# A state-space scan laid out as 8 batch rows x 16 states on the partitions, with its neighbouring stages cut into 4-step chunks

## The chip, the cores and the metric

The kernel runs on one core of a Trainium2 chip. A core has five engines that work from queues of their own: TensorE (PE, matrix products; its weight loads are listed as PEld), VectorE (DVE), ScalarE (ACT), GpSimd (POOL) and SyncE (SP, which here only starts DMA transfers). PE writes its products to PSUM, a small accumulator memory cut into banks; all other tiles are in SBUF, 128 partitions wide. The metric is the time of one execution in microseconds on the device, a median of several runs. Everything is in float32.

## The reference, cut to what matters

Two nets follow each other on x (128 sequences x 32 steps x 128 channels): a conditioning net and six layers of attention and feed-forward. The change is in the conditioning net alone:

```
xr, gate = split(x @ W_in.T)            # 256 channels each
xr = xr + t_emb[:, None, :]
xc = silu(causal_conv4(xr) + b_conv)    # along the 32 steps, each channel by itself
xn = layernorm(xc) * ln_g + ln_b
Bm, Cm, dt = split(xn @ W_xproj.T, 3)   # 16 states each
dt = tanh(dt @ W_dt.T + b_dt) * 0.01
Ad = 1 + dt * -tanh(A_log)
Bd = Bm * minimum(norm(xn), 1)
for each step t:                        # h: sequences x 16 states x 256 channels
    h = clip(h * Ad[t] + Bd[t] (x) xn[t], -10, 10)
    ys[t] = sum over states of Cm[t] * h
out = (ys + D * xn) * silu(gate) @ W_out.T
```

The loop is a true recurrence: with the clip in it, step t cannot start before step t-1 is clipped. One step handles 128 x 16 x 256 state values.

## The kernel before, in words

`cond_net` (lines 107 to 391) fills the stream `xT`, which holds channels on partitions and 4096 tokens along the free dimension; `ffn_net` (line 527) works on it in place. Both open their own pools of tiles, and those of `cond_net` close before those of `ffn_net` open.

`cond_net` works in three stages, one behind the other.

1. Lines 156 to 209, eight rounds of 16 sequences: load x (L161), transpose (L167), project (L172), add the embedding (L175), convolve with one ACT and three DVE operations (L183, L191), SiLU (L199); the gate likewise (L204, L205). Results have channels on partitions.
2. Lines 212 to 307, all 32 steps: transpose back to sequences on partitions (L220, L221), moments (L226, L227), normalise (L240), scale and shift (L249), transpose again (L260, L265), project to the 48 small values per token (L272, L279), squares for the norm (L283), then the small vectors Bd and Ad.
3. Lines 317 to 391, the scan. Sequences are on partitions, so h is a tile of 128 x 16 x 256, and Ad and Bd of one state are one value per partition. For each step, in groups of four states, ACT writes the products Bd (x) xn into a PSUM tile `u` with two buffers (L332), and DVE adds h_old * Ad (L339: one scalar_tensor_tensor of 128x256 for each of 16 states). After every eight states DVE clips 128x2048 values in one tensor_scalar (L349). For the read-out POOL builds 16 diagonal matrices of Cm (L355, four operations), and PE multiplies the 2 x 16 blocks of h with them and accumulates (L368), together with D * xn (L364). DVE multiplies by the gate (L373), and every fourth step PE projects (L382) and ACT copies to the stream (L391).

The order of instructions on an engine in these stages is that of the program, as the framework schedules it. `ffn_net` is different: it registers every step with a time in a `Plan` (line 394), which sorts them by time and ties each instruction to the one before it on its engine. The times set the order on each engine, nothing more: an engine starts its next instruction as soon as what it depends on is there. `ffn_net` starts with loads of weights (L449 to L478) and clearing two tiles on POOL (L440).

Other lines that the steps below refer to: L685 and L488 are tensor_scalar operations on POOL, L978 copies on POOL, L674, L691 and L743 tensor_tensor operations on POOL, all in `ffn_net`; L720 and L798 are its products on parts of the array (128 rows x 32 columns, and 32 rows x 64 columns), L817 its output projection of 256 columns.

Of the kernel before, what the change touches and what calls it, by code (L numbers as in the profile page):

```python
# [8 lines left out]
F32 = mybir.dt.float32  # L9
# [97 lines left out]
def cond_net(tc, x, cond, w_inT, w_xT, w_xdt, w_dtT, w_outT, ident, eps, pv, rv, stream):  # L107
    nc = tc.nc
    with ExitStack() as ctx:
        big = ctx.enter_context(tc.tile_pool(name="c_big", bufs=1))  # L110
        ps = ctx.enter_context(tc.tile_pool(name="c_ps", bufs=4, space=PSUM))

        wi = big.tile([128, 4, 128], F32, name="wi")
        nc.sync.dma_start(out=wi, in_=w_inT.rearrange("d (m c) -> d m c", c=128))
        wx = big.tile([128, 2, 3 * NS], F32, name="wx")
        nc.sync.dma_start(out=wx, in_=w_xT.rearrange("(k p) n -> p k n", p=128))
        wxd = big.tile([NS, C], F32, name="wxd")
        nc.scalar.dma_start(out=wxd, in_=w_xdt)
        wdt = big.tile([NS, NS], F32, name="wdt")
        nc.scalar.dma_start(out=wdt, in_=w_dtT)  # L120
        wot = big.tile([128, 2, 128], F32, name="wot")
        nc.sync.dma_start(out=wot, in_=w_outT.rearrange("(k p) n -> p k n", p=128))
        cd = big.tile([128, C], F32, name="cd")
        nc.scalar.dma_start(out=cd, in_=cond)


        gT = big.tile([128, 2, S, B], F32, name="gT")

        xcT = big.tile([128, 2, S, B], F32, tag="chan", name="xcT")

        condT = big.tile([128, 2, B], F32, name="condT")
        pc = ps.tile([128, 512], F32, tag="mm", name="pc")
        for ct in range(2):
            nc.tensor.transpose(
                pc[:, ct * 128 : (ct + 1) * 128], cd[:, ct * 128 : (ct + 1) * 128], ident
            )
        nc.vector.tensor_copy(condT, pc[:, :256].rearrange("p (k b) -> p k b", k=2))


        wc = big.tile([128, 2, 3 * NS], F32, name="wc")  # L140
        nc.vector.tensor_copy(wc[:, :, 0 : 2 * NS], wx[:, :, 0 : 2 * NS])
        pw = ps.tile([128, 512], F32, tag="mm", name="pw")
        for ct in range(2):
            nc.tensor.matmul(
                pw[:, ct * NS : (ct + 1) * NS],
# [950 lines left out]
```

## Time and profile before

| what | value |
|---|---|
| median of 3 runs | 3165.16 us (3161.58 to 3169.61) |
| the profiled execution, first to last instruction | 3171.8 us, that is 6.6 us above the median |
| busy: PE, PEld, DVE, ACT, POOL | 2994.4, 2033.4, 2632.2, 2201.3, 2114.7 us |
| conditioning net, stages 1 and 2 | about 0 to 145 us |
| conditioning net, scan | about 145 to 483 us |
| first attention product of the feed-forward net | 489.2 us |
| mean granted TensorE clock | 0.98 of full |

The page's 40 slices show the busy tenths of each engine; a slice is 79 us, so the conditioning net is the first six:

```profile
PE   6678886999999999999999999999999999999998
DVE  6699996888888888888888888888888888888884
ACT  6577773777776777777777767777777777677674
POOL 0144546777777777777777777777777777777772
PEclk9699998999999999999999999999999999999999
```

In the rows of instruction groups, a line reads: line of the kernel, engine, operation, output <- inputs, shapes, count, then total busy time, mean ns of one, and the idle time of the engine just before with what ended it. The mean of one can be longer than busy time over count, because consecutive operations overlap by some 80 ns. Profiled spans on POOL are rough.

### The profile page before, as it was taken

What the parts mean: (1) busy time and instruction counts of PE and PEld (TensorE: products, weight loads), DVE (VectorE), ACT (ScalarE), POOL (GpSimd) and SP (SyncE); (2) the same over time, 40 slices, a digit from 0 to 9 for tenths busy, and PEclk for the clock granted to TensorE, in tenths of its full rate; (3) what the DMA queues carried; (4) which work ended last, traced back from release to release, by engine and by line L of the source; (5) the groups of instructions that cost most, each with busy time, mean ns of one, the idle gap of its engine ahead of it and who ended that gap; (6) DMA issues with size and microseconds to landing.
All of it is one profiled execution on the core that took longest, in us unless ns stands there. A gap on an engine that the chain in (4) does not pass through costs nothing.

```text
span 3171.8 us, 105434 instructions
## 1 busy us (share of the span) xinstructions
PE 2994.4 (94%) x47942; PEld 2033.4 (64%) x47942; DVE 2632.2 (83%) x3607; ACT 2201.3 (69%) x2656; POOL 2114.7 (67%) x1560
## 2 busy tenths in 40 slices
PE   6678886999999999999999999999999999999998
PEld 3677773666666666666666666666666666666665
DVE  6699996888888888888888888888888888888884
ACT  6577773777776777777777767777777777677674
POOL 0144546777777777777777777777777777777772
PEclk9699998999999999999999999999999999999999
DMA  1000001000001000000000010000000000000000
GB/s 45 1 1 1 1 1 60 9 3 2 2 2 33 5 2 2 2 22 13 4 2 2 2 33 5 2 2 2 22 13 8 2 3 2 2 2 9 16 9 25
DMA packets 24586, 30.21 MB, mean 10 GB/s; under 512 B 1342, under 2 KB 22348, under 8 KB 23372
## 3 DMA queue, kind: packets, MB, share of 16 engines
q1 hardware_dynamic: 23644, 22.50, 2.3%
q8 instruction: 377, 6.18, 0.8%
q10 hardware_dynamic: 496, 0.97, 0.1%
q14 instruction: 69, 0.57, 0.1%
HBM read 21.36 MB, written 2.10 MB: 7 GB/s over the span
## 4 chain that ended last, share of the span: by engine, by line
PE 86%; DVE 5%; ACT 1%; POOL 1%; issue 1%; DMA 0%; DVEq 0%; POOLq 0%; ACTq 0%; SPq 0%
PE pq L644 20%; PE po L817 11%; PE pv L776 11%; PE pt L702 10%; PE av L798 8%; PE ph L923 8%; PE sim L720 6%; PE py L368 5%; PE pf L949 4%; DVE h L339 2%; DVE h L349 2%; PE pm L901 1%; PE pt L877 1%; POOL rot L674 1%; PE po L382 1%
## 5 line engine op out<-in xcount | busy, mean ns | idle before, releaser
L674 POOL TENSOR_TENSOR rot<-rot,tmp 128x512 f32<-128x512 f32 x768 | 956.5, 1272 | 16.8 <-DVE tmp L665 16.5
L644 PE MATMUL pq<-wq_t,xT 128*128 128x512 f32 x1536 | 714.3, 598 | 9.6 <-DMA wq_t<-in_wqkv_dram 6.6
L655 ACT ACTIVATE sq<-pq 128x1024 f32<-128x1024 f32 x384 | 393.5, 1025 | 473.2 <-DVE tmp L665 467.3
L665 DVE TENSOR_TENSOR rot<-pq,rt 128x1024 f32<-128x1024 f32 x384 | 468.0, 1219 | 190.7 <-PE pq L644 185.5
L743 POOL TENSOR_TENSOR sc<-sc,tb 128x1024 f32<-128x1024 f32 x96 | 227.2, 2367 | 406.3 <-DVE sc L734 291.3
L669 DVE TENSOR_REDUCE ssq<-sq 128x16 f32<-128x1024 f32 x384 | 465.5, 1212 | 8.4 <-ACT sq L655 4.2
L665 DVE TENSOR_TENSOR tmp<-pq,rt 128x1024 f32<-128x1024 f32 x384 | 466.3, 1214 | 0.0
L644 PEld LDWEIGHTS pq<-wq_t,xT 128*128 128x128 f32 x1536 | 278.3, 192 | 254.0 <-issue 239.3
L702 PE MATMUL pt<-ident,rot 128*128 128x128 f32 x3072 | 374.4, 275 | 24.6 <-POOL rot L691 22.3
L702 PEld LDWEIGHTS pt<-ident,rot 128*128 128x128 f32 x3072 | 344.3, 142 | 76.9 <-issue 28.6
L712 ACT COPY kd<-pt 64x1024 f32<-64x1024 f32 x384 | 387.0, 1008 | 4.9 <-PE pt L702 2.6
L817 PE MATMUL po<-oT,wo_t 128*128 128x256 f32 x1536 | 372.3, 385 | 0.8 <-DVE hid L936 0.5
L776 PE MATMUL pv<-wq_t,xT 128*128 128x512 f32 x768 | 362.9, 605 | 0.0
L691 POOL TENSOR_TENSOR rot<-rot,rn 128x1024 f32<-128x1024 f32 x192 | 361.6, 1905 | 0.1
L798 PEld LDWEIGHTS av<-at,v 32*64 32x64 f32 x24576 | 264.5, 130 | 113.8 <-issue 69.9
L763 POOL TENSOR_TENSOR sc<-sc,sm 128x1024 f32<-128x1024 f32 x96 | 184.0, 1916 | 227.7 <-DVE sm L759 215.7
L817 PEld LDWEIGHTS po<-oT,wo_t 128*128 128x128 f32 x1536 | 284.0, 190 | 80.2 <-issue 44.5
L355 POOL TENSOR_TENSOR dg<-ident,dbc 128x512 f32<-128x512 f32 x128 | 160.0, 1282 | 238.3 <-PE py L368 179.8
L368 PE MATMUL py<-dg,h 128*128 128x128 f32 x2048 | 248.8, 280 | 67.2 <-DVE h L349 67.2
L786 ACT COPY v<-pv 128x1024 f32<-128x1024 f32 x192 | 194.2, 1012 | 169.7 <-PE pv L776 169.7
L798 PE MATMUL av<-at,v 32*64 32x32 f32 x24576 | 286.1, 225 | 7.4 <-DVE at L769 4.9
L368 PEld LDWEIGHTS py<-dg,h 128*128 128x128 f32 x2048 | 240.5, 196 | 71.7 <-issue 71.2
(129 smaller groups left out, 4376.2 us busy)
## 6 DMA issues: line engine op xcount, KB each, us to landing
wq_t<-in_wqkv_dram SPq DMA_DIRECT2D x6, 1536.0 KB, 6.9
xl<-in_x_dram SPq DMA_DIRECT2D x16, 256.0 KB, 3.0
wo_t<-in_wo_dram SPq DMA_DIRECT2D x6, 512.0 KB, 5.0
out_dram<-xl SPq DMA_DIRECT2D x8, 256.0 KB, 3.0
w_t<-in_w_dram SPq DMA_DIRECT2D x6, 341.0 KB, 5.6
w_t<-in_w_dram SPq DMA_DIRECT2D x6, 128.0 KB, 2.9
rv<-in_rvec_dram ACTq DMA_DIRECT2D x1, 656.0 KB, 4.4
wi<-in_w_inT_dram SPq DMA_DIRECT2D x1, 256.0 KB
```

The lines of the kernel that those rows point to most:

```text
L368: nc.tensor.matmul(py[:, cs], h[:, d, cs], dg[:, d, :], start=False, stop=(d == NS - 1))
L644: self.nc.tensor.matmul(self.acc[i, c][:, n, :], self.shifted(i), self.wq_t[:, o : o + 512], start=True, stop=True,)
L655: self.nc.scalar.activation(sq.rearrange("p h d -> p (h d)"), pq, AF.Square)
L665: nc.vector.tensor_tensor(out, pq, table, ALU.mult)
L669: self.nc.vector.tensor_reduce(self.ssq[:, i, c * H : (c + 1) * H], sq, AX.X, ALU.add)
L674: self.nc.gpsimd.tensor_tensor(rot[:, :, a : a + 32], rot[:, :, a : a + 32], tmp[:, :, b : b + 32], ALU.add)
L691: self.nc.gpsimd.tensor_tensor(kr, kr, rk, ALU.mult)
L702: nc.tensor.transpose(pt[:, n * 128 : (n + 1) * 128], rf[:, o : o + 128], self.net.ident)
L712: self.nc.scalar.copy(self.net.kd[i][rows, :, :, r, :], ptc[rows])
L776: self.nc.tensor.matmul(self.acc["v", i][:, n, :], self.shifted(i), self.wq_t[:, o : o + 512], start=True, stop=True,)
L798: self.nc.tensor.matmul(self.av[j // 2][64 * r : 64 * r + 64, j % 2, o : o + 32], self.v[i][toks, h * DH : (h + 1) * DH], self.at[toks, i ...
L817: self.nc.tensor.matmul(self.po, self.wo_t[:, c, :], self.oT[:, :, :, c, :].rearrange("p j i q -> p i j q"), start=(c == 0), stop=(c == HP ...
```

## The change

Stages 1 and 2 and the scan become steps of a `Plan`, as in the feed-forward net. The 32 time steps are cut into 8 chunks of 4. A `Chunk` does for its 4 steps and all 128 sequences what stages 1 and 2 did (its convolution takes the last three columns of the chunk before), and its steps have times up to 57 units ahead of its first scan step; a scan step has 8 units.

In a `Scan` step the state lies otherwise. There are 16 groups of 8 sequences; in a group, the 128 partitions are 8 sequences x 16 states, and the free dimension is the 256 channels. Per step:

- The terms Bd (x) xn are 16 products on PE, in two halves: a stationary block of 32 sequences x 128 (8 sequences x 16 states, zero where the sequence differs) times xn of these 32 sequences. Four products with different rows of the array go to four PSUM banks. The tile has one buffer.
- DVE updates with 16 scalar_tensor_tensor operations of 128x256, one for each group, with Ad as one value per partition.
- The clip is four tensor_scalar operations of 128x1024 on POOL.
- The read-out is 16 products with a stationary block of 128 x 32 (Cm placed so that each sequence sums its 16 states), four side by side in the array's columns. DVE adds D * xn, POOL multiplies by the gate, PE transposes, ACT copies, and every fourth step PE projects and ACT stores.

To make the blocks, ACT multiplies the 48 small values of a chunk by eight masks (`masked`) and four more (`spread`); PE turns Ad and Cm to the new partitions (`select`), and POOL places Cm (`placed`). The layer norm's scale and shift move from DVE to POOL, the normalisation from DVE to ACT, and the 48 small values are projected from the SiLU output before normalisation, with the norm folded into the weights and applied afterwards. The constants for this are made once at the start. `cond_net` keeps its place and its pools still close before the feed-forward net's open. Dots stand for what is left out.

```diff
-def cond_net(tc, x, cond, w_inT, w_xT, w_xdt, w_dtT, w_outT, ident, eps, pv, rv, stream):
...
+QT = 4
+NQ = S // QT
+STEP = 8
+GROUPS = B // 8
+class Cond:
...
+        self.cm = [big.tile([128, QT * 4, 160], F32, name=f"cm{i}") for i in range(2)]
+        for cm in self.cm:
+            nc.gpsimd.memset(cm.rearrange("p r w -> p (r w)"), 0.0)
...
+        plan = Plan(tc)
+        self.chunks = [Chunk(self, q) for q in range(NQ)]
+        for q in range(NQ):
+            self.chunks[q].plan(plan, q * QT * STEP)
+        for t in range(S):
+            Scan(self, t).plan(plan, t * STEP)
+        plan.emit()
...
+    def load(self, q):
+        xl = self.xl[q] = self.wk.tile([128, QT, D], F32, tag="cxl", name="cxl")
+        self.nc.sync.dma_start(out=xl, in_=self.x[:, q * QT : (q + 1) * QT, :])
+class Chunk:
...
+    def plan(self, plan, t0):
+        def at(time, step, *args):
+            plan.at(t0 + time, lambda: step(*args))
+        if self.q >= 2:
+            at(-93.31, self.load)
+        at(-56.94, self.tokens)
+        at(-55.40, self.copied)
+        at(-55.18, self.project, 0)
+        at(-55.06, self.conditioned, 0)
+        at(-53.81, self.project, 1)
+        at(-50.61, self.tap, 0)
+        at(-50.35, self.conditioned, 1)
+        at(-49.00, self.taps, 0, 0)
+        at(-45.12, self.tap, 1)
+        at(-42.59, self.taps, 1, 0)
+        at(-40.58, self.taps, 0, 1)
+        at(-38.43, self.gates, 0)
+        at(-37.76, self.taps, 1, 1)
+        at(-36.22, self.gated, 0)
+        at(-34.49, self.taps, 0, 2)
+        at(-33.64, self.taps, 1, 2)
+        at(-33.40, self.silu, 0)
+        at(-31.72, self.gates, 1)
+        at(-31.05, self.silu, 1)
+        at(-29.65, self.gated, 1)
+        at(-29.39, self.back, 0)
+        at(-29.21, self.back, 1)
+        at(-28.57, self.moments, 0)
+        at(-28.35, self.moments, 1)
+        at(-25.96, self.deviation)
+        at(-25.18, self.inverse)
+        at(-24.33, self.normalised, 0)
+        at(-23.89, self.normalised, 1)
+        at(-23.02, self.scaled, 0)
+        at(-20.95, self.offset, 0)
+        at(-20.24, self.norm, 0)
+        at(-18.50, self.scaled, 1)
+        at(-18.46, self.small, 0)
+        at(-17.23, self.small, 1)
+        at(-17.04, self.offset, 1)
+        at(-14.94, self.skip)
+        at(-14.93, self.small_out)
+        at(-13.89, self.norm, 1)
+        at(-13.71, self.norm_root)
+        at(-13.45, self.inputs)
+        at(-12.49, self.masked)
+        at(-6.15, self.select)
+        at(-5.55, self.spread, 0)
+        at(-3.67, self.decay)
+        at(-3.59, self.outputs)
+        at(-1.51, self.decays)
+        at(1.69, self.placed)
+        at(3.82, self.spread, 1)
+        at(52.20, self.project_out)
+        at(53.63, self.store)
...
+    def conditioned(self, ct):
+        nc = self.nc
+        if ct == 0:
+            self.xp = self.wk.tile([128, 2, QT + 3, B], F32, tag="xp", name="xp")
+            if self.q == 0:
+                nc.gpsimd.memset(self.xp[:, :, 0:3, :], 0.0)
+            else:
+                before = self.net.chunks[self.q - 1].xp
+                nc.gpsimd.tensor_copy(self.xp[:, :, 0:3, :], before[:, :, QT : QT + 3, :])
+        nc.vector.tensor_tensor(
+            self.xp[:, ct, 3:, :],
+            self.acc.pop(("r", ct)).rearrange("p (t b) -> p t b", b=B),
+            self.net.condT[:, ct, :].unsqueeze(1).to_broadcast([128, QT, B]),
+            ALU.add,
+        )
...
+    def taps(self, ct, k):
+        acc = self.acc["c", ct]
+        self.nc.vector.scalar_tensor_tensor(
+            acc, self.xp[:, ct, k : k + QT, :], self.weight(ct, k), acc, ALU.mult, ALU.add
+        )
...
+    def moments(self, u):
+        nc = self.nc
+        if u == 0:
+            self.stats = self.wk.tile([128, QT, 6], F32, tag="cst", name="cst")
+            self.mv = self.wk.tile([128, QT, 2], F32, tag="cmv", name="cmv")
+        for k in range(2):
+            nc.vector.bn_stats(self.stats[:, 2 * u + k, :], self.acc["t", u][:, k * C : (k + 1) * C])
+        for k in range(2):
+            nc.vector.bn_aggr(self.mv[:, 2 * u + k, :], self.stats[:, 2 * u + k, :])
...
+    def affine(self, u, o, op):
+        xn = self.xn[:, 2 * u : 2 * u + 2, :]
+        row = self.net.rv[:, o : o + C].unsqueeze(1).to_broadcast([128, 2, C])
+        self.nc.gpsimd.tensor_tensor(xn, xn, row, op)
...
+    def masked(self):
+        self.m = self.wk.tile([128, QT * 3, 8, NS], F32, tag="m", name="m", bufs=1)
+        src = self.dbc.rearrange("p t (k d) -> p (t k) d", d=NS)
+        for l in range(8):
+            self.nc.scalar.activation(
+                self.m[:, :, l, :], src, AF.Copy, scale=self.net.in_group[:, l : l + 1]
+            )
+    def spread(self, u):
+        if u == 0:
+            self.e = self.wk.tile([128, QT, 4, 128], F32, tag="e", name="e")
+        src = self.m.rearrange("p (t k) l d -> p t k (l d)", k=3)[:, :, 0, :]
+        for j in (2 * u, 2 * u + 1):
+            self.nc.scalar.activation(
+                self.e[:, :, j, :], src, AF.Copy, scale=self.net.quarter[:, j : j + 1]
+            )
+    def select(self):
+        ps = self.psel = self.net.bank("psel")[:, : QT * 2 * GROUPS].rearrange(
+            "p (k t g) -> p k t g", k=2, t=QT
+        )
+        m = self.m.rearrange("p (t k) l d -> p t k (l d)", k=3)
+        for t in range(QT):
+            for k in range(2):
+                self.nc.tensor.matmul(
+                    ps[:, k, t, :], m[:, t, 1 + k, :], self.net.of_group, start=True, stop=True
+                )
...
+    def placed(self):
+        self.cm = self.net.cm[self.q % 2]
+        dst = self.cm.rearrange("p r (m w) -> p r m w", w=40)[:, :, :, 0:8]
+        part = [128, QT * 4, 4, 8]
+        self.nc.gpsimd.tensor_tensor(
+            dst,
+            self.cs.rearrange("p t (r m) -> p (t r) m", m=4).unsqueeze(3).to_broadcast(part),
+            self.net.row_b.unsqueeze(1).unsqueeze(1).to_broadcast(part),
+            ALU.mult,
+        )
...
+class Scan:
...
+    def plan(self, plan, t0):
+        def at(time, step, *args):
+            plan.at(t0 + time, lambda: step(*args))
+        at(-1.59, self.terms, 0)
+        at(0.06, self.update, 0, 0)
+        at(0.33, self.update, 0, 1)
+        at(2.40, self.clip, 0, 0)
+        at(5.23, self.terms, 1)
+        at(5.83, self.update, 1, 0)
+        at(5.94, self.clip, 0, 1)
+        at(6.16, self.update, 1, 1)
+        at(7.68, self.clip, 1, 0)
+        at(10.84, self.clip, 1, 1)
+        at(13.52, self.read, 0)
+        at(14.38, self.read, 1)
+        at(15.75, self.skip)
+        at(19.83, self.gate)
+        at(22.42, self.turn)
+        if self.t % 2 == 1:
+            at(23.35, self.turned)
+    def terms(self, i):
+        ch, k = self.chunk, self.k
+        self.u = self.net.ps.tile([128, 4, 2, C], F32, tag="u", name="u", bufs=1)
+        for j in range(2):
+            for r in range(4):
+                rows = slice(32 * r, 32 * r + 32)
+                self.nc.tensor.matmul(
+                    self.u[:, r, j, :],
+                    ch.e[rows, k, 2 * i + j, :],
+                    ch.xn[rows, k, :],
+                    start=True,
+                    stop=True,
+                )
+    def update(self, i, w):
+        nc, net, ch = self.nc, self.net, self.chunk
+        if i == 0 and w == 0:
+            net.h[self.t] = self.wk.tile([128, 2, 4, 2, C], F32, tag="h", name="h")
+        h = net.h[self.t]
+        if self.t == 0:
+            nc.vector.tensor_copy(h[:, i, 2 * w : 2 * w + 2], self.u[:, 2 * w : 2 * w + 2])
+            return
+        for r in (2 * w, 2 * w + 1):
+            for j in range(2):
+                g = 4 * r + 2 * i + j
+                nc.vector.scalar_tensor_tensor(
+                    h[:, i, r, j, :],
+                    net.h[self.t - 1][:, i, r, j, :],
+                    ch.a[:, self.k, g : g + 1],
+                    self.u[:, r, j, :],
+                    ALU.mult,
+                    ALU.add,
+                )
+    def clip(self, i, w):
+        h = self.net.h[self.t][:, i, 2 * w : 2 * w + 2].rearrange("p r j c -> p (r j c)")
+        self.nc.gpsimd.tensor_scalar(h, h, -10.0, 10.0, ALU.max, ALU.min)
+    def read(self, i):
+        ch = self.chunk
+        if i == 0:
+            self.y = self.net.ps.tile([128, 512], F32, tag="y", name="y", bufs=1)
+        h = self.net.h[self.t]
+        for j in range(2):
+            for r in range(4):
+                m = 2 * i + j
+                self.nc.tensor.matmul(
+                    self.y[32 * r : 32 * r + 32, 0:C],
+                    ch.cm[:, self.k * 4 + r, 32 * m : 32 * m + 32],
+                    h[:, i, r, j, :],
+                    start=(m == 0),
+                    stop=(m == 3),
+                )
+    def skip(self):
+        self.z = self.wk.tile([128, C], F32, tag="z", name="z")
+        self.nc.vector.tensor_tensor(self.z, self.y[:, 0:C], self.chunk.xd[:, self.k, :], ALU.add)
+    def gate(self):
+        self.nc.gpsimd.tensor_tensor(self.z, self.z, self.chunk.g[:, self.k, :], ALU.mult)
...
```

## The prediction

> **What bounds the kernel now.** I first cut the span into stages (busy time of each engine in each stretch: busy us and count, then the granted TensorE clock). The conditioning net ends near 482.8 us; the feed-forward net behind it is not edited.
>
> ```profile
> 0.00:76.00 76.00, 45.23 (x113) 21.59 (x114) 50.01 (x77) 48.21 (x52) 5.06 (x28) 0.92 0.16 47
> 76.00:145.00 69.00, 42.88 (x255) 42.28 (x253) 51.74 (x114) 36.95 (x103) 10.36 (x8) 0.65 0.00 1
> 145.00:482.80 337.80, 270.69 (x2200) 256.85 (x2200) 304.07 (x592) 245.57 (x527) 149.61 (x120) 0.97 0.00 1
> ```
>
> DVE is busy 304 of the 337.8 us of the scan (90%), PE 271, ACT 246, POOL 150; ahead of it lie 145 us in which no engine leads. The groups of instructions by form give the prices:
>
> ```profile
> L339 DVE SCALAR_TENSOR_TENSOR h<-h,ad,u 128x256 f32<-128x256 f32 x496 | 202.4, 473 | 3.5 <-ACT u L332 3.5
> L349 DVE TENSOR_SCALAR h<-h 128x2048 f32<-128x2048 f32 x64 | 95.4, 1490 | 7.5 <-ACT h L326 5.4
> L373 DVE TENSOR_TENSOR z<-py,gT 128x256 f32<-128x256 f32 x32 | 13.6, 425 | 20.7 <-PE py L368 20.5
> L191 DVE SCALAR_TENSOR_TENSOR acc<-xp,pv,acc 128x512 f32<-128x512 f32 x48 | 33.9, 747 | 1.0 <-ACT acc L183 0.6
> ...
> L674 POOL TENSOR_TENSOR rot<-rot,tmp 128x512 f32<-128x512 f32 x768 | 956.5, 1272 | 16.8 <-DVE tmp L665 16.5
> L691 POOL TENSOR_TENSOR rot<-rot,rn 128x1024 f32<-128x1024 f32 x192 | 361.6, 1905 | 0.1
> L743 POOL TENSOR_TENSOR sc<-sc,tb 128x1024 f32<-128x1024 f32 x96 | 227.2, 2367 | 406.3 <-DVE sc L734 291.3 <-DVE sd L895 115.0
> L685 POOL TENSOR_SCALAR rn<-rn 128x64 f32<-128x64 f32 x96 | 35.1, 366 | 27.2 <-ACT rn L680 27.2
> L978 POOL COPY full<-xT 64x496 f32<-64x496 f32 x8 | 4.8, 598 | 36.2 <-DVE last L957 35.9
> L488 POOL TENSOR_SCALAR cg<-cen,pv 128x128 f32<-128x128 f32 x6 | 3.7, 612 | 0.0
> ...
> L978 POOL COPY full<-last 64x16 f32<-64x16 f32 x8 | 1.7, 213 | 0.0
> ```
>
> The timeline of one step (start, duration, engine) shows how they queue:
>
> ```profile
> 255.97 2.04 DVE L339 SCALAR_TENSOR_TENSOR h<-h,ad,u 128x256 f32<-128x256 f32 x5
> 258.04 1.82 DVE L349 TENSOR_SCALAR h<-h 128x2048 f32<-128x2048 f32 x1
> 259.78 3.21 DVE L339 SCALAR_TENSOR_TENSOR h<-h,ad,u 128x256 f32<-128x256 f32 x8
> 263.02 1.23 DVE L349 TENSOR_SCALAR h<-h 128x2048 f32<-128x2048 f32 x1
> 265.86 0.42 DVE L373 TENSOR_TENSOR z<-py,gT 128x256 f32<-128x256 f32 x1 [0.44 <-PE py L368]
> 266.20 2.04 DVE L339 SCALAR_TENSOR_TENSOR h<-h,ad,u 128x256 f32<-128x256 f32 x5
> ```
>
> The period is 266.20 - 255.97 = 10.23 us, of which DVE is busy 9.74: sixteen updates at (3.21 - 0.08)/8 = 0.39 (the last one's end does not overlap the next), 6.25, two clips of 1.23 and 1.82, one read-out product of 0.42. So **DVE bounds the scan**, and 32 x 10.2 + about 11 us at its two ends make up the 338. Last, the chain of waits shows how the stage is joined to the next:
>
> ```profile
> 480.62 2.00 PE po L382 x4
> 482.76 6.30 DMA wq_t<-in_wqkv_dram
> 489.19 3.77 PE pq L644 x4
> ```
>
> The last output product releases the load of the first attention weights, which PE waits for. The change leaves that joint: all pools of the net still close together. Everything from 482.8 on (3171.8 - 482.8 = 2689.0 us) is therefore carried over.
>
> **The change, part by part.**
>
> *The 145 us ahead of the scan* shrink to set-up and the first chunk alone; chunks 1 to 7 go beside the scan. Set-up: the trace's first matmul waits until 9.56 us for DMA; the new constants add about eight small hops between engines (four transposes of 0.28, copies of 0.6, small DVE operations of 0.2), to some 14 us. The first chunk is a chain, from rows of the same form: four transposes 1.1, copy 0.6, projection 0.85 (512 columns, as at 13 us), two sums 0.69 each, six taps 0.75 each, two SiLU 1.09 and a table load 1.28, transposes 1.1, moments 2.25 (12.5 + 5.5 us over 32), square root with load 1.5, reciprocal and offset 0.8, four normalisations 0.48 each, POOL scale and shift 4 x 1.27, squares 4 x 0.60, three small DVE operations 0.7, eight masks 0.4 each, spreads 2 x 0.8, tanh with load 1.5: 34 us, and 4 us for chunk 1 in between. The loads of x stay eight of 256 KB on SP (3.0 us to landing); all but two are now issued some 36 us ahead of their use with nothing queued before them: nothing, or 3 us where one is late. The scan then starts at about 14 + 38 = 52 us. After the last update come clip, read-out, sum, gate, two transposes, copy, two products of 0.6: 6 us. **Ends together: 58 us.**
>
> *DVE per step.* The updates keep their form (128x256, SBUF, a pointer, PSUM) and their count: 16 x 0.39 = 6.25. Clips leave: -3.05. The read-out sum stays at 0.42. New beside it, per 4-step chunk: two sums 1.38, six taps 4.24 (33.9/48 each), moments 2.25, small ones 1.5 = 9.4, or 2.35 a step. Sum 9.02.
>
> *ACT per step* loses 16 x 0.47 = 7.4 us of products. Per chunk it has copies 0.6 + 1.2, taps 1.6, SiLU 4.3, normalisations 1.9, squares 2.4, masks 3.2, spreads 3.3, stores 1.5, small 1.0, and four table loads of 1.28 (SiLU, square root and tanh alternate): 26 us, 6.5 a step. It is off the path, with 3 us to spare.
>
> *PE per step* loses 34 products of 128 columns and gets 16 of 32 rows x 128 columns (terms) and 16 of 128x32 (read-out), 256 wide, plus 1.7 us of chunk work (40 products and transposes). Such a product alone is 372.3/1536 = 0.24 us; the 32-row and 32-column forms of the attention run together at 0.012 and 0.016 us for 32 and 64 columns, two to four times below serial pace, so 8 terms take 0.9 (weight loads of 0.117 one behind another) to 1.9 us. PE needs 4 to 9.8 us. I take 5.5.
>
> *The new waits.* The term tile has a single buffer: DVE finishes eight updates, PE starts eight terms, DVE goes on. Hop, weight load and first product are 0.05 + 0.15 + 0.38 + 0.05 = 0.63 us, twice a step; where terms run serially, the fifth adds 0.6. What is queued on DVE between the two halves covers it: by the plan's times each first gap holds 1.4 to 2.25 us of chunk work and each second one the 0.42 of the read-out sum and up to 0.9. If that cover is late, up to 2 x 1.25 = 2.5 a step is lost. On PE the read-out of step t-1 stands between the two blocks of terms, so a late clip of the last piece holds the next step's first terms, and with them DVE.
>
> *POOL per step* loses the diagonals (4 x 1.28) and gets four clips of 128x1024, **the price that the trace lacks**. Around them: gate 0.73 (between 455 ns for 128 and 1272 for 512 elements), and per chunk scale and shift 5.1, skip 2.4, placing 1.3, carry-over copy 0.8: 9.6, or 2.4. So POOL = 4C + 3.1. Low end of C: the COPY rows grow by (598 - 213)/480 = 0.80 ns per element; 0.366 + 960 x 0.80 = **1.14 us**. High end: the straight line through the two TENSOR_SCALAR rows, (612 - 366)/64 = 3.84 ns per element, gives **4.05**. That line leaves 120 ns of fixed cost where COPY shows 200, and its second row reads a pointer and the first an immediate, as the clip does; so part of the difference should be the pointer. The two-input rows of the same size are 1.91 and 2.37. I take the nearest kind, one streamed input with immediates: 1.2 to 1.5, POOL 7.9 to 9.1, just under DVE. I keep both ends. The balance with DVE lies at C = (9.7 - 3.1)/4 = 1.65.
>
> The Trainium skill speaks on both sides here: its page GPSIMD Engine Reference, section Engine selection, calls GPSIMD the wrong place for elementwise work with two inputs (about half of VectorE's speed) but roughly at line rate with one, and its cycle accounting states 1.03 cycles per element for bodies of at most two operations, an estimate of 1024 x 1.03/1.2 = 0.88 us and a fixed part; by that POOL would need some 7 us a step and DVE stay the bound, while by the TENSOR_SCALAR line POOL would need 19.3. No row here shows a long one-input operation with two constants, so no run yet agrees or disagrees.
>
> *Port.* In the step above the clip that ran beside POOL took 1.82, the other 1.23: 0.6 us lost. Six taps per chunk have two SBUF inputs and may meet it: 0 to 6 x 0.6/4 = 0.9 a step. With the uncovered part of the term waits I put 0.7 on DVE's 9.02: **9.7 a step**.
>
> The Trainium skill (SBUF — State Buffer, Who interferes with whom) says that a VectorE instruction with two SBUF inputs holds off a GpSimd one that reads SBUF, and the other way round, for the whole instruction; by it a tap could wait for a full clip, 6 x 1.3/4 = 2 a step at worst, and the updates, with one input in PSUM, not at all.
>
> *Clock.* It was 0.65 at 76 to 145 us, 1.00 late in the scan and 0.85 after the joint (482.8 to 600). With less PE work in the scan it may be lower at the joint; at 0.65 for 60 us PE-bound work would lose 15 us, and as much can be gained if it is not cut at all. I put 0.
>
> **Sum.** 58 + 32 x 9.7 = 368 in place of 482.8: -114 us on the profiled 3171.8, which gives 3057. The median of the runs, 3165.2, is 6.6 lower: **3051**.
>
> **Rivals.** In general the time is 3165.2 - 482.8 + 58 + 32 x step = 2740 + 32 x step.
> (1) *The term buffer's cover is late*: step 9.0 + 1.3 to 2.5 = 10.3 to 11.5, 3070 to 3108. For it: engines take work in written order, and chunk work waits on others. Against: a chunk runs six steps ahead.
> (2) *POOL becomes the bound, mildly*: C between 1.65 and 2.5, as the two-input rows of that size have; at 1.91 the step is 10.7, 3082; at 2.37, 12.6, 3143.
> (3) *Slower: the clip on POOL costs as the TENSOR_SCALAR rows' line says.* The step that loses all is (482.8 - 58)/32 = 13.3, so it decides from C = 2.55. At 2.9: 14.7, 3210. At 4.05: 19.3, 3358. For it: both rows of that operation lie on the line, and no POOL row of it is cheap. Against: the fixed costs above.
> (4) *It doesn't do what it says*: the chunks run not beside the scan but ahead of its parts; then the 145 us stay, and 9.7 - 2.35 + 0.5 = 7.85 a step gives 3165 - 338 + 32 x 7.85 + 10 = 3088. This is unlikely, as nothing but the engines' order ties them.
>
> **Chances.** Forecast (step 9.0 to 10.3) 0.43, its own range 3028 to 3070; rivals 1 and 4 0.14; rival 2 0.10; rival 3 0.30; between, within 0.3% (9.5 us, about what a measurement can tell from no change) 0.03. Faster 0.67, same 0.03, slower 0.30. The range starts at 3015 and must take in about half of rival 3; C up to 3.3, a step of 16.3, ends at 3260.
>
> **What would show it.** After: the scan's start near 52 us and its end near 368; DVE over 90% busy between, POOL 80 to 95%; updates still 0.39 each; the clip's row on POOL below 1.65 us. If POOL is near 100% and DVE waits for it, rival 2 or 3 holds and the clip's mean tells which; if DVE waits for the term products on PE while POOL has gaps, rival 1. The forecast is wrong if C is above 1.65 or if the feed-forward part is not 2689 us.

## The result

The changed kernel takes 3316.3 us (median of 4 runs, 3316.1 to 3317.7) against 3163.8 us before (now four runs): a ratio of 1.048 (95% interval 1.046 to 1.050). It is **slower by some 152 us**, where 114 us of gain were forecast and 3260 us was the end of the range. The profiled execution spans 3314.3 us.

The same cut into stages as before, now at the scan's first update (48.9 us) and at the load that begins the feed-forward net (625.1 us); busy us and counts in the order PE, PEld, DVE, ACT, POOL, then the granted clock:

```profile
0.00:48.90 48.90, 26.04 (x105) 17.66 (x106) 21.12 (x51) 23.47 (x46) 16.52 (x21) 0.85 0.16 52
48.90:625.10 576.20, 324.39 (x2508) 173.47 (x2508) 274.07 (x685) 135.70 (x286) 553.75 (x208) 0.74 0.01 2
625.10:3314.30 2689.20, 2633.28 (x45376) 1712.53 (x45376) 2226.36 (x2824) 1871.65 (x1978) 1948.21 (x1404) 0.99 0.03 10
```

The 145 us ahead of the scan have become 49, and the feed-forward part is 2689.2 us, as carried over. The whole loss is in the middle row: 576 us for a scan of 338. There POOL is busy 553.8 of 576.2 us (96%) and DVE only 274. The groups that answer to those of before:

```profile
L660 POOL TENSOR_SCALAR h<-h 128x1024 f32<-128x1024 f32 x128 | 466.6, 3645 | 11.3 <-DVE h L644 1.7
L649 DVE SCALAR_TENSOR_TENSOR h<-h,a,u 128x256 f32<-128x256 f32 x496 | 203.0, 476 | 264.1 <-POOL h L660 217.2 <-PE u L630 46.9
...
L485 POOL TENSOR_TENSOR cxn<-cxn,rv 128x512 f32<-128x512 f32 x32 | 40.6, 1270 | 11.0 <-ACT cxn L474 9.6
...
L683 POOL TENSOR_TENSOR z<-z,g 128x256 f32<-128x256 f32 x32 | 23.4, 732 | 3.8 <-DVE z L680 1.8
...
L680 DVE TENSOR_TENSOR z<-y,xd 128x256 f32<-128x256 f32 x32 | 13.4, 418 | 13.9 <-PE y L670 13.6
```

One clip (L660) takes 3645 ns. 128 of them are 466.6 us, more than the whole scan took before. The updates (L649) still cost 203.0/496 = 0.41 us, but DVE stood idle 217.2 us in front of them for a clip, and 46.9 for terms. The chain of waits in the middle of the scan runs over POOL alone, one operation behind the other with some 0.07 us between:

```profile
279.69 3.62 POOL h L660
283.31 0.06 issue
283.37 3.63 POOL h L660
287.00 0.07 issue
287.07 1.27 POOL cxn L485
288.35 0.69 POOL z L683
289.04 1.23 POOL cxn L485
290.26 0.08 issue
290.35 4.07 POOL h L660
```

So a step is 4 x 3.645 + 3.1 = 17.7 us of POOL. Read back from the span, with the 58 us that the prediction gave the two ends, it is (625.06 - 58)/32 = 17.7. What is left to find is why a clip costs 3.6 us and not 1.2, and whether that is all.

### The profile page after: what moved, and what is told of

Same layout as the page of the kernel before. It is cut to its first block, busy times and chain, and to the rows that moved or that the text cites. A ratio compares the mean times of both kernels' runs of the same rounds, so it can differ in the third digit from the quotient of the medians.

```text
span 3314.3 us, 105209 instructions
## 1 busy us (share of the span) xinstructions
PE 2983.7 (90%) x47988; PEld 1903.7 (57%) x47988; DVE 2521.6 (76%) x3559; ACT 2030.8 (61%) x2309; POOL 2518.5 (76%) x1633
## 4 chain that ended last, share of the span: by engine, by line
PE 79%; POOL 15%; DVE 3%; issue 2%; ACT 1%; DMA 0%; SPq 0%; DVEq 0%; POOLq 0%; ACTq 0%
PE pq L932 19%; POOL h L660 12%; PE po L1105 11%; PE pv L1064 10%; PE pt L990 10%; PE av L1086 8%; PE ph L1211 7%; PE sim L1008 5%; PE pf L1237 4%; PE pm L1189 1%; POOL cxn L485 1%; PE pt L1165 1%; DVE h L649 1%; POOL z L683 1%; POOL xd L572 0%
## 5 line engine op out<-in xcount | busy, mean ns | idle before, releaser
L943 ACT ACTIVATE sq<-pq 128x1024 f32<-128x1024 f32 x384 | 393.2, 1024 | 474.7 <-DVE tmp L953 460.9
L660 POOL TENSOR_SCALAR h<-h 128x1024 f32<-128x1024 f32 x128 | 466.6, 3645 | 11.3 <-DVE h L644 1.7
L649 DVE SCALAR_TENSOR_TENSOR h<-h,a,u 128x256 f32<-128x256 f32 x496 | 203.0, 476 | 264.1 <-POOL h L660 217.2
L670 PE MATMUL y<-h,cm 128*32 128x256 f32 x1024 | 122.2, 514 | 212.9 <-POOL h L660 212.8
```

The costliest lines, as they stand in the source:

```text
L660: self.nc.gpsimd.tensor_scalar(h, h, -10.0, 10.0, ALU.max, ALU.min)
L943: self.nc.scalar.activation(sq.rearrange("p h d -> p (h d)"), pq, AF.Square)
```

## The experiments

Theory A: POOL's throughput, set by the clip's price, makes the step. Rivals: B, the single-buffered terms; C, the delay from update to clip to next update; D, POOL held off by DVE at a port that they share. "Joint" is the start of the load of the first attention weights in the profiled execution, "step" is (joint - 58)/32. Ratios are to the kernel before, in runs on the same chip.

| run | edit of the changed kernel | median us | ratio (95%) | joint | step |
|---|---|---|---|---|---|
| changed kernel | | 3316.3 | 1.048 (1.046-1.050) | 625.1 | 17.7 |
| e1 | no clip | 3055.0 | 0.964 (0.962-0.967) | 363.3 | 9.5 |
| e2 | clip on DVE | 3116.4 | 0.983 (0.980-0.986) | 421.1 | 11.3 |
| e3 | half on DVE, half on POOL | 3129.2 | 0.988 (0.985-0.991) | 433.5 | 11.7 |
| e5 | three quarters on DVE | 3140.4 | 0.991 (0.989-0.994) | 448.7 | 12.2 |
| e6 | as e3, but all on DVE in one step of four | 3112.6 | 0.983 (0.981-0.985) | 417.9 | 11.2 |
| e7 | one bound only, on POOL | 3208.9 | 1.013 (1.010-1.016) | 515.0 | 14.3 |
| e8 | as e5, convolution on PE | 3153.1 | 0.995 (0.993-0.996) | 450.3 | 12.3 |
| e9 | clip on DVE, two term buffers | 3150.9 | 0.995 (0.992-0.998) | 455.0 | 12.4 |
| e10 | as e9, convolution on PE | 3186.9 | 1.006 (1.004-1.008) | 492.1 | 13.6 |
| e11 | *kernel before*, clip on POOL | 3441.7 | 1.086 (1.083-1.089) | 744.4 | |
| e13 | clip on POOL, min before max | **3072.9** | 0.970 (0.968-0.971) | 378.9 | 10.0 |
| e14 | as e13, convolution on PE | 3100.9 | 0.979 (0.977-0.981) | 402.2 | 10.8 |
| e15 | *kernel before*, clip on POOL, min before max | 3149.6 | 0.994 (0.992-0.996) | 455.9 | |

**Is it the clip, and what lies under it?** No bound is applied in e1; the scan's plan loses four lines.

```diff
-        at(2.40, self.clip, 0, 0)
-        at(5.94, self.clip, 0, 1)
-        at(7.68, self.clip, 1, 0)
-        at(10.84, self.clip, 1, 1)
```

> The clip of the state is left out; all else is as in the changed kernel. Theory A (POOL's throughput: four clips of 3.65 us plus 3.1 us of other POOL work make its 17.7 us per step) expects POOL to drop to 3.1 us a step and DVE to become the bound: 9.0 us of work plus up to 0.7 of gaps, so 49 us to the scan's start + 32 x (9.0 to 9.7) + 10 + 2689 = 3036 to 3060 us. Rival B (the single-buffered term tile stops DVE twice a step) expects 10.3 to 11.5 us a step even without clips, 3078 to 3116 us.

Measured 3055.0 us (this kernel does not clip, so its values are not the reference's). DVE is busy 272.5 of the 314.3 us from 49 us to the joint (87%), a step is 9.5 us. The clip on POOL is more than the whole loss, and beneath it lies a step near the forecast's, with DVE the busiest engine. B alone (10.3 or more) is excluded, though DVE still waits 29.0 us for terms, 0.9 a step.

**The clip back on DVE (e2)**, in one operation over `h[:, i]` (128x2048) for each half; the four POOL clips go as in e1.

```diff
+        at(0.40, self.clip_half, 0)
+        at(6.20, self.clip_half, 1)
...
+        self.nc.vector.tensor_scalar(h, h, -10.0, 10.0, ALU.max, ALU.min)
```

> The clip is done on DVE, as before the change: two operations of 128x2048 per step, each right behind the eight updates of its half. Theory A: DVE 9.0 + 2 x 1.23 to 1.5 = 11.5 to 12.0 us, plus gaps up to 0.3, so 3116 to 3142 us. Rival B: the clips now lie where DVE waits for the next terms only in part, 12.5 us or more a step, over 3150 us.

Measured 3116.4 us, at the lower end for A. Everything in the change but the clip's move gains 55 us of the 3171.7 that the kernel before takes on the same chip, 1.7%.

**Half and half (e3)** keeps the two POOL clips of the second half and does the first on DVE.

```diff
-        at(2.40, self.clip, 0, 0)
-        at(5.94, self.clip, 0, 1)
+        at(0.40, self.clip_half, 0)
```

> The first half of the state is clipped on DVE (one operation of 128x2048), the second half on POOL (two of 128x1024). Theory A: POOL 2 x 3.65 + 3.1 = 10.4, DVE 9.0 + 1.2 to 1.8 = 10.2 to 10.8; a step of 10.6 to 11.3 us, 3087 to 3110 us, below the version with all clips on DVE. Rival C (not POOL's throughput but the way of an update through POOL's queue, that is, the latency from update to clip to next update, sets the step): half of DVE's 217 us of waiting for clips stays, about 14 us a step, near 3196 us.

Measured 3129.2 us. C (3196) is out, but A's 3087 to 3110 was missed as well: neither POOL (336.9 of the 384.5 us from 49 us to the joint) nor DVE (325.4) is full.

**The price by itself (e4)**: POOL operations on 64 to 2048 elements of 128 partitions, behind the changed kernel's last instruction.

```diff
+            nc.gpsimd.tensor_scalar(b, b, -10.0, 10.0, ALU.max, ALU.min)
+            nc.gpsimd.tensor_scalar(b, b, -10.0, None, ALU.max)
+            nc.gpsimd.tensor_scalar(b, b, pv[:, 0:1], None, ALU.mult)
+            nc.gpsimd.tensor_copy(b, b)
```

The timeline (start, duration, engine, line); L102 is max and min with constants, L103 max alone, L104 a mult with a pointer, L105 a copy, L107 mult and add with constants, L108 and L109 a lone mult and a lone min:

```profile
3314.23 0.43 POOL L102 TENSOR_SCALAR ba<-ba 128x64 f32<-128x64 f32 x1
...
3314.74 0.37 POOL L103 TENSOR_SCALAR ba<-ba 128x64 f32<-128x64 f32 x1
3315.21 0.45 POOL L104 TENSOR_SCALAR ba<-ba,pv 128x64 f32<-128x64 f32 x1
...
3327.95 3.63 POOL L102 TENSOR_SCALAR ba<-ba 128x1024 f32<-128x1024 f32 x1
3331.66 2.77 POOL L103 TENSOR_SCALAR ba<-ba 128x1024 f32<-128x1024 f32 x1
3334.53 2.85 POOL L104 TENSOR_SCALAR ba<-ba,pv 128x1024 f32<-128x1024 f32 x1
3337.44 1.04 POOL L105 COPY ba<-ba 128x1024 f32<-128x1024 f32 x1
...
3358.67 1.05 POOL L107 TENSOR_SCALAR ba<-ba 128x1024 f32<-128x1024 f32 x1
3359.80 2.77 POOL L108 TENSOR_SCALAR ba<-ba 128x1024 f32<-128x1024 f32 x1
3362.65 2.77 POOL L109 TENSOR_SCALAR ba<-ba 128x1024 f32<-128x1024 f32 x1
```

> The changed kernel with a row of POOL operations behind its end, while DVE is idle: tensor_scalar with two constants, with one constant and with one pointer, and copies, for 64 to 2048 elements per partition; at 1024 also mult and add, one mult, one min, and a tensor_tensor; then three clips on DVE. Theory A1 (the price is that of the operation itself) expects the clip of 1024 at 3.6 us with DVE idle and a line of 3.4 ns per element. Rival D (POOL is held off by DVE at the port they share) expects 1.1 to 1.5 us at 1024 with DVE idle. If the second operation is what costs, the form with one constant takes about half; if the pointer costs, its row lies above that with one constant by a fixed amount.

With DVE idle the clip of 1024 elements takes the same 3.63 us, so D is out as its cause. The pointer costs 0.08 us. A lone operation costs (2.77 - 0.37)/960 = 2.5 ns per element, the pair max and min (3.63 - 0.43)/960 = 3.3, a copy 0.83. And mult and add, a pair too, runs at the copy's pace.

**One bound only (e7)**: the upper bound is left out, so this kernel too computes something else than the reference.

```diff
-        self.nc.gpsimd.tensor_scalar(h, h, -10.0, 10.0, ALU.max, ALU.min)
+        self.nc.gpsimd.tensor_scalar(h, h, -10.0, None, ALU.max)
```

> All clips on POOL as in the changed kernel, but only the lower bound is applied (the upper one is left out). The price of POOL's operation by itself was 2.77 us with one constant and 3.63 with two at 1024 elements. Theory A (throughput): 4 x 2.77 + 3.1 = 14.2 us a step, 2748 + 454 = 3202 us. If it were the number of hand-overs between DVE and POOL and not their duration that counts, no change from 3316 us.

Measured 3208.9 us, step 14.3 against 14.2: throughput, not the number of hand-overs.

**Why the splits fell short (e5, e6).** e5 is e3 with one more quarter (128x1024) on DVE, so that one is left to POOL; e6 is e3, but all on DVE in the second of each four steps. On top of e3's edit:

```diff
-        at(7.68, self.clip, 1, 0)
+        at(5.95, self.clip_dve, 1, 0)
```

```diff
-        at(7.68, self.clip, 1, 0)
-        at(10.84, self.clip, 1, 1)
+        if self.k == 1:
+            at(6.20, self.clip_half, 1)
+        else:
+            at(7.68, self.clip, 1, 0)
+            at(10.84, self.clip, 1, 1)
```

> Three quarters of the clip on DVE (128x2048 and 128x1024), the last quarter on POOL. Theory A with uneven load: DVE 11.45 - 0.55 = 10.9 us a step, POOL 3.65 + 3.1 = 6.8 on average and 10.3 in the step that holds scale and shift, so POOL never leads: 2748 + 32 x 10.9 to 11.1 = 3097 to 3103 us. If any clip on POOL costs by its delay alone, no better than all on DVE, 3116 us or more.

> The halves are split between DVE and POOL in three of four steps; in the step of each chunk that also holds POOL's scale and shift (5.1 us) DVE clips all. Theory A with uneven load (the even split was slower than its means say because POOL needs 7.3 + 0.7 + 5.9 = 13.9 us in one of four steps while DVE needs 10.5): 10.7 in three steps, 11.5 in the fourth, 10.9 on average, near 3097 to 3105 us. If the split suffers from the delay of POOL's clips in every step, (3 x 11.85 + 11.45)/4 = 11.75, near 3124 us.

e5 became slower, 3140.4 us, and missed. The groups of the clip on DVE and of the taps, first in e2 and then in e5 (there up to 430 us, 31 of the 32 clips):

```profile
L662 DVE TENSOR_SCALAR h<-h 128x2048 f32<-128x2048 f32 x64 | 84.6, 1322 | 2.2
...
L388 DVE SCALAR_TENSOR_TENSOR conv<-xp,pv,conv 128x512 f32<-128x512 f32 x48 | 36.2, 778 | 0.2 <-ACT conv L378 0.2
```

```profile
L663 DVE TENSOR_SCALAR h<-h 128x2048 f32<-128x2048 f32 x31 | 45.2, 1458 | 1.1
L388 DVE SCALAR_TENSOR_TENSOR conv<-xp,pv,conv 128x512 f32<-128x512 f32 x48 | 44.4, 949 | 0.2 <-ACT conv L378 0.2
```

The mean tap grows from 778 to 949 ns and the clip of 2048 from 1322 to 1458, so from 49 us to the joint DVE is busy 353.0 us (e2: 347.5), although a quarter of the clip went to POOL, some 18 us (the 0.55 a step of the expectation). It is not POOL's clip that lengthens the taps, nor how busy POOL is: with POOL 96% busy in the changed kernel the mean tap is 816 ns, with no clip at all (e1) 930. What counts is the POOL operation that a tap meets. Of e5's 48 taps, 11 started while POOL ran the skip (L572) or the placing (L563); these took 1.27 to 2.61 us, and the median of all is 0.744.

And DVE's wait for terms grows from 12.1 to 31.2 us, as the clip that covered it is gone. The other runs agree: without a clip on DVE between the last update of a step and the first of the next it is 29.0 (e1), 30.5 (e3) and 26.9 us (e13).

e6 went somewhat over half of the way that the uneven load had promised (3129 to 3113). DVE's wait for POOL fell from 8.8 us in e3 to nothing, as that theory has it, but its wait for terms fell as much (30.5 to 21.8), since in one step of four the clip on DVE covers it again. So the uneven load explains a part of e3's miss, and the uncovered terms another.

**More work off DVE (e8)**: on top of e5's edit, the taps become four accumulating products with diagonal weights (`dw`, the taps' weights times the unit matrix); SiLU reads them from PSUM and adds the bias.

```diff
-        at(-49.00, self.taps, 0, 0)
...
+        at(-34.00, self.convolved, 0)
...
+        pv = self.acc["c", ct] = self.net.bank("pcv")
+        for k in range(4):
+            self.nc.tensor.matmul(
+                pv,
+                self.net.dw[:, 4 * ct + k, :],
```

> As the version with a quarter of the clip on POOL, and the convolution is moved from ACT and DVE to PE: four accumulating products with diagonal matrices per 128 channels, 512 columns each. Theory A (DVE is the bound once POOL is relieved): DVE loses 4.24/4 = 1.06 us a step, 9.8 to 10.3 us a step, 3062 to 3078 us. If PE, which gets 8 x 0.44/4 = 0.9 us a step more in line with the terms, holds the terms back, no gain over the quarter version.

A miss, and slower than e5: what came is the expectation's second case, no gain. Between 100 and 300 us DVE is busy only some 80%, PE 85%, and DVE waits 42.7 us for terms in all.

**Two term buffers (e9, e10).** The tile of four banks becomes two of two banks, each filled from two row groups (and the second spread of a chunk is put earlier, for its terms); the clip is e2's. e10 is e9 with e8's convolution.

```diff
-        self.u = self.net.ps.tile([128, 4, 2, C], F32, tag="u", name="u", bufs=1)
+        u = self.u[i, w] = self.net.ps.tile([128, 2, 2, C], F32, tag="u", name="u", bufs=2)
...
-            for r in range(4):
+            for r in (2 * w, 2 * w + 1):
```

> All clips on DVE, and the term tile of four banks with one buffer becomes tiles of two banks with two buffers, each filled by four products, so that terms are made while DVE updates. Rival B, as a part of the whole (DVE waits for terms): with all clips on DVE it waited 12.1 us in 32 steps, 0.38 a step; without that wait 11.1 us a step, 3100 to 3108 us. If two rows of the array at a time make the terms too slow, no gain over 3116 us.

> All clips on DVE, convolution on PE, two buffers for the terms. Theory A with its two additions (DVE operations beside POOL ones are longer; an uncovered term wait stops DVE): no clip on POOL meets DVE, DVE has 11.0 - 1.06 = 9.95 us of work a step and little waiting, 10.1 to 10.6 us a step, 3071 to 3087 us. If PE is the bound with the convolution (it was busy 10.4 us a step in the quarter version with the convolution), 10.8 us or more a step, over 3094 us.

Both slower. The term products, in e2 and in e9:

```profile
L628 PE MATMUL u<-cxn,e 32*128 32x256 f32 x1024 | 93.6, 489 | 90.6 <-DVE h L647 87.0 <-DVE h L642 3.6
```

```profile
L631 PE MATMUL u<-cxn,e 32*128 32x256 f32 x1024 | 175.4, 500 | 22.0 <-DVE h L651 20.6 <-DVE h L646 0.3
```

Two row groups side by side instead of four take 175.4 us of PE's time against 93.6. A part of this is the clock: from 49 us to the joint 0.75 was granted in e9 and 0.84 in e2. At 0.74, in the changed kernel, four side by side took 105.4 us:

```profile
L630 PE MATMUL u<-cxn,e 32*128 32x256 f32 x1024 | 105.4, 542 | 31.2 <-DVE h L649 27.4 <-DVE csd L453 2.6 <-ACT e L526 1.2
```

So at about the same clock two cost 1.7 times what four cost. PE is busy 92% of the time from 49 us to the joint in e9, ahead of DVE's 85%, and in e10 95 to 97% between 100 and 400 us. The ten runs of e9 scatter from 3126 to 3173 us; why is not known.

**The clip's move by itself (e11)**: one word in L349 of the kernel before.

```diff
-                        nc.vector.tensor_scalar(hh, hh, -10.0, 10.0, ALU.max, ALU.min)
+                        nc.gpsimd.tensor_scalar(hh, hh, -10.0, 10.0, ALU.max, ALU.min)
```

> The kernel before the change with only one part of it: its two clips of 128x2048 per step go from DVE to POOL. Theory A: POOL 2 x 7.08 (measured by itself) + 4 x 1.28 = 19.3 us a step in place of a step of 10.23, 3164 + 32 x 9.1 = 3455 us. Rival C (delay through POOL, not its throughput): the two halves follow each other on POOL while DVE works on the other, 3.2 + 7.1 us for a half, near 10.5 a step, 3175 us.

Measured 3441.7 us, near A's 3455, far from C's 3175. A's price was a little high, since the diagonals (L355) take 1.06 us each here; their 1.28 was a mean from before, where some meet a clip of DVE and take 2.0. With it a step of POOL is 2 x 7.07 + 4 x 1.06 = 18.4 us, and the joint moved by just that: 10.23 + (744.4 - 482.8)/32 = 18.4.

**Other forms (e12)**, in the same place as e4's, with other pairs of operations, of which five here:

```diff
+        nc.gpsimd.tensor_scalar(b, b, 2.0, 1.0, ALU.mult, ALU.add)
+        nc.gpsimd.tensor_scalar(b, b, 1.0, 0.5, ALU.add, ALU.mult)
...
+        nc.gpsimd.tensor_scalar(b, b, 1.0, 10.0, ALU.mult, ALU.min)
+        nc.gpsimd.tensor_scalar(b, b, 0.0, 10.0, ALU.add, ALU.min)
+        nc.gpsimd.tensor_scalar(b, b, 10.0, -10.0, ALU.min, ALU.max)
```

The timeline: L101 is mult and add, L102 add and mult, L104 mult and min, L105 add and min, L106 min and max, L107 mult and add with two pointers:

```profile
3315.27 1.04 POOL L101 TENSOR_SCALAR ba<-ba 128x1024 f32<-128x1024 f32 x1
...
3316.39 1.04 POOL L102 TENSOR_SCALAR ba<-ba 128x1024 f32<-128x1024 f32 x1
...
3318.65 3.63 POOL L104 TENSOR_SCALAR ba<-ba 128x1024 f32<-128x1024 f32 x1
3322.37 3.64 POOL L105 TENSOR_SCALAR ba<-ba 128x1024 f32<-128x1024 f32 x1
3326.09 1.04 POOL L106 TENSOR_SCALAR ba<-ba 128x1024 f32<-128x1024 f32 x1
3327.24 1.19 POOL L107 TENSOR_SCALAR ba<-ba,pv 128x1024 f32<-128x1024 f32 x1
```

> The changed kernel with further POOL operations behind its end, DVE idle, 1024 elements: two constants as mult and add (1.05 us in the first series), add and mult, mult and mult, mult and min, add and min, min and max, two pointers with mult and add, then mult and add at 2048 and 64 elements, and two clips on DVE. Theory: only mult and add run at the copy's pace of 0.83 ns per element and every form with min or max at 3.6 us; if it is the pair of constants and not the operation that is quick, mult and mult are quick too and the order of min and max matters.

The theory fell: **min and then max takes 1.04 us, max and then min 3.63**. The constants and the values are the same. Mult and mult (L103, not shown) took 1.05.

**The order swapped in the changed kernel (e13)**, one line:

```diff
-        self.nc.gpsimd.tensor_scalar(h, h, -10.0, 10.0, ALU.max, ALU.min)
+        self.nc.gpsimd.tensor_scalar(h, h, 10.0, -10.0, ALU.min, ALU.max)
```

> The changed kernel with the two operations of the clip in the other order: min with 10, then max with -10; the values are the same. Theory A (POOL's throughput, set by the form of the clip): C = 1.04, POOL 4 x 1.04 + 3.1 = 7.3 us a step, so DVE is the bound as without clips, 9.5 to 9.8 us a step, 2748 + 304 to 314 = 3052 to 3062 us. If the order does not matter beside the scan, 3316 us; if POOL clips cost by their delay or at the port whatever their length, 11 us a step or more, over 3100 us.

```profile
L649 DVE SCALAR_TENSOR_TENSOR h<-h,a,u 128x256 f32<-128x256 f32 x496 | 199.4, 473 | 27.0 <-PE u L630 26.9
L660 POOL TENSOR_SCALAR h<-h 128x1024 f32<-128x1024 f32 x128 | 138.2, 1080 | 81.6 <-DVE h L649 57.1 <-PE ptc L421 11.2 <-DVE h L644 3.9
...
L388 DVE SCALAR_TENSOR_TENSOR conv<-xp,pv,conv 128x512 f32<-128x512 f32 x48 | 52.2, 1109 | 0.2 <-ACT conv L378 0.2
```

Measured 3072.9 us: 243 us under the changed kernel, 0.970 of the kernel before, the best of all that clip. The clip is 1080 ns beside the scan, POOL idles in front of it for DVE (57.1 us), and DVE is busy 291.8 of the 329.9 us from 49 us to the joint. It is 11 us above the end of A's range, which was worked out from e1, the kernel without clips. Against e1 DVE is busy 19.3 us more: 8.7 in the taps (930 to 1109 ns) and 10.6 in three small operations, which now end just behind the POOL operation that they start in: L510 (225 to 957 ns) behind a clip, L507 mostly behind the skip, L455 behind the carry-over copy. The taps, too, are held up by the quick clip, as they were not by the slow one. A tap that starts within a clip, first in the changed kernel, then here:

```profile
92.77 3.62 POOL L660 TENSOR_SCALAR h<-h 128x1024 f32<-128x1024 f32 x1
93.48 0.87 DVE L388 SCALAR_TENSOR_TENSOR conv<-xp,pv,conv 128x512 f32<-128x512 f32 x1
```

```profile
119.81 1.04 POOL L660 TENSOR_SCALAR h<-h 128x1024 f32<-128x1024 f32 x1
119.94 1.45 DVE L388 SCALAR_TENSOR_TENSOR conv<-xp,pv,conv 128x512 f32<-128x512 f32 x1
```

All 16 taps of e13 that start within a clip end 0.54 us after its end (119.94 + 1.45 = 121.39, the clip ends at 120.85). The 31 that start within a max-and-min clip in the changed kernel take 0.74 to 0.88 us, one of them 1.08, and none waits for the clip's end.

**What comes next (e14, e15).** e14 is e13 with e8's convolution; e15 is the kernel before with the cheap form on POOL in L349:

```diff
-                        nc.vector.tensor_scalar(hh, hh, -10.0, 10.0, ALU.max, ALU.min)
+                        nc.gpsimd.tensor_scalar(hh, hh, 10.0, -10.0, ALU.min, ALU.max)
```

> As the version with min before max, and the convolution on PE. DVE has 1.06 us a step less, 8.5; POOL 7.3; PE gets 0.9 more, near 9. If DVE alone is the bound, 8.9 to 9.2 us a step, 3033 to 3042 us; if PE and the single-buffered terms take over, 9.5 us or more, no gain over the version with min before max.

> The kernel before the change with its two clips of 128x2048 per step on POOL, as min and then max. Theory A: POOL 2 x 1.90 + 4 x 1.28 = 8.9 us a step, DVE 6.7, ACT 7.5: 9.0 to 9.6 us in place of 10.23, 3125 to 3145 us. With max before min the same kernel took 3442 us.

e14: no gain, 3100.9 us; DVE's work falls to 256.7 us, but it waits 44.9 us for terms (e13: 26.9), with PE at 295.8 of the 353.2 us from 49 us to the joint. Which of the convolution's products hold up which terms was not tried. e15: 3149.6 us, somewhat above A's range; DVE then waits 44.6 us for ACT's products, and only 17 us are gained where the whole change with the same form of clip (e13) gains 94.

## Why the prediction was wrong

**The step that failed is one price**: "I take the nearest kind, one streamed input with immediates: 1.2 to 1.5". It carried the 0.80 ns per element of a copy over to max and min with constants; e4 measured 3.63 us. The bound from above, 4.05, was near, and by accident: its two rows are a lone max (L685) and a lone mult with a pointer (L488), not a pair as the clip is. The 3.84 ns per element mixed a pointer (0.08 us) with the 2.5 of a lone operation, while the true line for the pair max and min is 3.3. That both rows lie on the line, named in its favour, says nothing, as two points always do.

The argument against that bound (copy has 200 ns fixed, the line leaves 120) was sound, but it was not followed to its end. The COPY rows' line gives 200 + 64 x 0.80 = 251 ns for 64 elements, and L685 takes 366. The low end of 1.14 put these 115 ns to the fixed cost; put to the elements they make (366 - 200)/64 = 2.6 ns each and 2.86 us for 1024, an estimate close to the 2.77 that a lone max then measured, and above the limit of 2.55. So a row of before did speak against 1.2 to 1.5. No row showed what a pair costs or that its order matters: with min written first the same clip takes 1.04 us, so 1.2 to 1.5 would have been nearly right for that form.

**Rival 3 came, by its formula**: 2740 + 32 x 17.7 = 3306 against 3316.3. It had 0.30, and the range was cut at C = 3.3, inside its own bounds; with ends at 1.14 and 4.05 and only neighbours as evidence, the high half deserved more.

**Most other steps held, one of them by luck.** The scan's start: 48.9 for 52 us. The feed-forward part: 2689.2 for 2689.0, although the granted clock in the scan was 0.74 and not 0.97; the 0 put for it was right here. POOL's other work: e7 gave 14.3 for 4 x 2.77 + 3.1 = 14.2. DVE's step came out near the 9.7: 9.5 without clips, 10.0 with the cheap clip. So e13's 3073 us stands against the forecast's 3051, just outside its own range (3028 to 3070).

But the two terms of the 9.7 erred in opposite directions, and that they met is luck. The work was put too high, 9.02 a step: in e1 it is 272.5/32 = 8.5, with longer taps than were priced. 9.4/32 = 0.3 of this is a slip in the sum, which counts eight chunks beside the scan although the first lies ahead of it. The 0.7 for the port and for the waits was too low: DVE waited 29.0/32 = 0.9 a step for terms in e1 and 26.9/32 = 0.8 in e13 (inside the 2.5 at most that the prediction named), and in e13 the port took (1109 - 747) x 48/32 = 0.54 in the taps, inside the 0 to 0.9 given, and 10.6/32 = 0.33 in small operations, which were put at nothing. PE's 5.5 a step was too low as well (253.2/32 = 7.9 in e13); it was inside the 4 to 9.8 named.

**Rivals 1, 2 and 4** did not come. e7, with a clip of 2.77 us, lies just beyond rival 2 (up to 2.5) and in rival 3: 3209 us, slower than before, which fits the limit of 2.55.

The Trainium skill's figure for GPSIMD (GPSIMD Engine Reference, cycle accounting: 1.03 cycles per element for at most two operations) is met by some forms and not by others. Min and max, mult and add took 1.04 us for 1024 elements, near the estimate that the prediction worked out from that page, 0.88 us and a fixed part; max and min took 3.63 and even a lone max 2.77. The measurement decides: the number of operations does not tell the price.

Its rule on the port (SBUF — State Buffer, Who interferes with whom) is met by some POOL operations and not by others. In e13 a tap, with two SBUF inputs, that starts within a quick clip ends 0.54 us behind it, and one that starts within POOL's two-input operations (L563, L572, L683) 0.55 us behind; the updates, with one input in PSUM, kept 473 to 476 ns in all runs. Both are as the page says. The clip as max and min reads SBUF too, and by the page a tap would wait for its end; the 31 taps within one in the changed kernel did not (0.74 to 0.88 us, one 1.08). The measurement decides here as well.

## What to carry to other kernels

An operation that moves to another engine is priced by a row of that engine with the same operation in the same form; where there is none, measure it by itself first, in both orders of its two operations. An engine that takes work off the bound can hold it up in other places: the gain is not the work moved, as e5 and e13 show, and which operations meet decides, not how busy the engine is. And a part that was covered by the work that is moved, here the wait for terms, comes back.

## What the runs showed that was not expected

- On POOL, tensor_scalar with two constants takes 1.04 or 1.05 us for 1024 elements as mult and add, add and mult, mult and mult, or min and max, but 3.63 as max and min, mult and min, or add and min. Why is open; other pairs were not tried.
- A single operation (max, min or mult with one constant) takes 2.77 us, more than twice the quick pairs.
- The quick clip holds up DVE's taps until it ends, and the slow forms let them run: 16 of 16 taps in e13 against 0 of 31 with max and min (changed kernel) and 0 of 31 with a lone max (e7, 0.74 to 1.11 us). Why is open.
- The 256-column products on 32 rows take 0.10 us of PE each four side by side (105.4 us for 1024 records, granted clock 0.74) and 0.17 two side by side (175.4 us, 0.75).
